# A perceiver block's graph stage: half of the batches sorted by GpSimd transfers with computed addresses, in place of one-hot products

## The chip, the core and the metric

One core of a Trainium2 chip runs the whole program. The metric is the device time of one execution in microseconds, as the median of several runs. The engines are TensorE (PE, with its weight loads PEld apart), VectorE (DVE), ScalarE (ACT), GpSimd (POOL) and SyncE (SP), which issues nearly all transfers of the kernel before. Each takes its instructions in order and waits for others through semaphores.

## The reference, cut to what matters

The input x has 16 batches of 32 channels and 512 nodes; the context gives three coordinates per node. The block adds three parts to x in turn: a graph stage, a state-space scan and a feed-forward part. Only the graph stage is touched. Its core, per layer:

```
keys  = [morton(q), morton(q_swapped), hilbert(q), hilbert(q_swapped)]
order = [argsort(k, axis=1) for k in keys]              # 4 methods, per batch
start = max(0, i - 5); end = min(N, i + 6)              # a window of 10 in sorted order
inds  = order[min(start + arange(10), end - 1)]
neigh = feats[inds]                                     # features of the window
x     = concat(center, neigh - center), channels permuted over methods, cast to float16
scores = einsum('bihd,bjhd->bhij', x, x) / sqrt(32)     # per node, 10 x 10, heads of 32
out   = softmax(scores) @ x                             # then a linear layer, a conv, instance norm, max
```

So each layer needs the node features of every batch put into the sorted order of each of four methods. There are two layers; the second takes the first one's output. The order is the same in both.

## The kernel before, in words

The work is split in four groups `g` of four batches (4 x 32 channels fill the 128 partitions) and two layers, eight passes in the order (0,L1) (1,L1) (0,L2) (2,L1) (1,L2) (3,L1) (2,L2) (3,L2). L1 has 32 output channels per batch, L2 has 64. A pass has 43 blocks of 12 nodes, 344 blocks in all, run as a software pipeline: the main loop (`for it in range(len(blocks) + 5)`, at the end of `graph_part`) issues for each `it` one step each of several blocks. In the order of the program: the exponential of block it-1 (`expo`, L870 and L875), `turn` of it-3 (L896), `scores` of it (L846, L853), `rest` and `reduce` of older blocks (L960 to L969), `greatest` (`c`, L862), `mapped` (L915, L920), `sums` (`z`, L882), then `steps`, which advances the preparation of the next pass, then `shares` of it-1 (`rz` on VectorE, L888, and `EN` on GpSimd, L890), `outputs` of it-3 (L943), and `differences` of block it+6 (`DD` on GpSimd, L811, and its copies `DX`, four transfers on SP per three blocks, L821). `EN` is thus read two iterations after it is issued, `DD` six after; `LEAD` is 6. Nothing reorders the instructions (`manual_schedule`).

The sorted position of each node comes from comparisons of keys: a TensorE product (L540) and a sign with accumulated sum on ScalarE (L541) give `rank`, one instruction pair for 128 nodes of one batch and method. `rank` holds 2 x position - 511. There are 256 such pairs; 32 are done before the first preparation starts, and `ranks_of(b)` tells how many must be done before batch b can be placed.

A preparation `prep(g, layer)` is a generator that brings one pass's features into sorted order. It stores the source in DRAM (`dC`), turns it on TensorE into `FT` (nodes on partitions, L641 and L643), splits `FT` into three bfloat16 parts `F3` (L648, L650), makes the linear part of the centre (`share`), and then for each of the four batches and four chunks of 128 nodes makes four one-hot matrices on VectorE (L751, one per method, 128x512) and multiplies the three parts by each on TensorE (L705, 12 products of 32 columns by 512). After four chunks ScalarE copies the result (L712), SP stores it to DRAM (L716), loads the centres `crep` (four transfers, L681) and loads the sorted features back as `fs`, spread over partitions by head (four transfers, L725). Each call of `next` runs it to its next `yield`: two one-hots per step.

`steps` calls the next pass's preparation once per block, or twice while more steps are left than `NGRP - LEAD - SPARE - gi`, which is 34 less the block number `gi`. The counts come from `PREP`: 49 steps for a preparation of L1, 46 for L2. From the second pass on it starts at block 4 at the earliest; while the former pass's end (`tails`) still runs, one step per block or none. A preparation that yields False (ranks not there yet) does not count a step. The first preparation runs alone, before block 1, with a rank comparison per step.

Of the kernel before, what the change touches and what calls it, by code (L numbers as in the profile page):

```python
# [8 lines left out]
F32 = mybir.dt.float32  # L9
F16 = mybir.dt.float16  # L10
# [13 lines left out]
M = 4  # L24
# [21 lines left out]
NHT = 16  # L46
LR = 18
LEAD = 6
PREP = (49, 46, 42)
SPARE = 3  # L50


# [325 lines left out]
def graph_part(nc, tc, cx, I, dram, id32, ones, xt, F0, layernorm_steps, rstd_steps, scan_input):  # L378
# [62 lines left out]

    EN = [keep.tile([P, NI, 32], F32, name=f"EN{k}") for k in range(2)]
    rank = keep.tile([P, 4, M, B], F32, name="rank")
    F1 = [keep.tile([P, D], F32, name=f"F1_{g}") for g in range(NBG)]

    W3 = gc.tile([P, 4, P], F32, name="W3")
# [100 lines left out]
    def ranks_of(b):  # L547

        return FIRST // 2 + HALF * (b + 1) if b < 4 else 4 * M * (b + 1)
# [70 lines left out]
    def later_tile(n):  # L620
        return ps_1.tile([P, D], F32, tag="misc", bufs=2, name=f"kd{n}")

    KEPT = ()
    kept = {}
    transfers = []

    def prep(g, layer, early=False):


        L, co, npair, WA, WC, HB = layers[layer]  # L630
        key = f"{L}_{g}"
        src = F1[g] if layer else F0[:, g]
        if layer == 0:
            yield from layernorm_steps(sm, src, xt[:, g], f"g{g}")
            yield
        dC = dram.tile([P, D], F32, name=f"dC{key}")
        nc.sync.dma_start(out=dC, in_=src)

        pf = ps_1.tile([P, 4, P], F32, tag="misc", bufs=2, name=f"pf{key}")
        for c in range(4):  # L640
            nc.tensor.transpose(pf[:, c], src[:, c * P:(c + 1) * P], id32)  # L641
        FT = wk.tile([P, 4, P], F32, tag="FT", name=f"FT{key}", bufs=1)
        nc.scalar.copy(FT, pf)  # L643
        yield

        F3 = [wk.tile([P, 4, P], BF16, tag=f"F3_{k}", name=f"F3_{k}{key}", bufs=1) for k in range(3)]
        for k in range(3):
            nc.vector.tensor_copy(F3[k], FT)  # L648
            if k < 2:
                nc.vector.tensor_tensor(FT, FT, F3[k], ALU.subtract)  # L650
                yield
        at_hand = layer == 1 and g in KEPT

        def share():

            c16 = wk.tile([P, D], F16, tag="c16", name=f"c16{key}", bufs=1)
            nc.vector.tensor_copy(c16, src)
            yield
            c32 = wk.tile([P, D], F32, tag="c32", name=f"c32{key}", bufs=1)
            nc.vector.tensor_copy(c32, c16)  # L660
            yield
            yield
            hc = wk.tile([P, npair, D], F32, tag="hc", name=f"hc{key}")
            for pr in range(npair):
                ph = ps_1.tile([P, D], F32, tag="misc", bufs=2, name=f"ph{key}_{pr}")
                nc.tensor.matmul(ph, lhsT=WC[:, pr], rhs=c32, start=True, stop=True)
                nc.scalar.activation(hc[:, pr], ph, AF.Identity, bias=HB)
                yield
            made[key][2] = hc

        made[key] = [None, None, None]
        if not at_hand:
            yield from share()

        crep = big.tile([P, 4, D], F32, tag="crep", name=f"crep{key}", bufs=2)
        later = []

        def centre(b):
            for m in range(M):
                r = 32 * b + 8 * m  # L680
                nc.sync.dma_start(  # L681
                    out=crep[r:r + 8], in_=dC[32 * b:32 * b + 32].rearrange("(h c) n -> c h n", h=4)
                )

        if early:
# [12 lines left out]
        fs = big.tile([P, 4, D + 4], F32, tag="fs", name=f"fs{key}", bufs=2)  # L698
        pend = []

        def place():
            b, c, ohs, pp = pend.pop(0)
            for m in range(M):
                for k in range(3):
                    nc.tensor.matmul(  # L705
                        pp[32 * m:32 * m + 32, :], lhsT=F3[k][:, c, 32 * b:32 * b + 32], rhs=ohs[m // 2][:, m % 2],
                        start=(c == 0 and k == 0), stop=(c == 3 and k == 2),
                    )
# [12 lines left out]

            def spread():
                for m in range(M):
                    r = 32 * b + 8 * m
                    nc.sync.dma_start(  # L725
                        out=fs[r:r + 8, :, :D], in_=dS[32 * m:32 * m + 32].rearrange("(h c) n -> c h n", h=4)
                    )

            later.append([2, store])

        for b in range(4):
            while ranked[0] < ranks_of(4 * g + b):
                yield False
            pp = None
            for c in range(4):
                if c == 0:
                    pp = ps_1.tile([P, D], F32, tag="pp", name=f"pp{key}_{b}")
                if at_hand and len(pend) == 2:
                    place()
                    tick()  # L740
                    yield
                ohs = [
                    wk.tile([P, 2, D], BF16, tag="oh", name=f"oh{key}_{b}_{c}_{i}", bufs=4) for i in range(2)
                ]
                for i, oh in enumerate(ohs):
                    if at_hand:
                        transfers.append((oh, kept[g, b, c, i]))
                        continue
                    for j in range(2):
                        m = 2 * i + j  # L750
                        nc.vector.tensor_scalar(  # L751
                            oh[:, j], it2, rank[:, c, m, 4 * g + b:4 * g + b + 1], None, ALU.is_equal
                        )
                    if layer == 0 and g in KEPT:
                        kept[g, b, c, i] = dram.tile([P, 2, D], BF16, name=f"k{key}_{b}_{c}_{i}")

                        def keep_it(to=kept[g, b, c, i], oh=oh):
                            nc.scalar.dma_start(out=to, in_=oh)

                        later.append([1, keep_it])  # L760
                    if i == 0:
                        tick()
                        yield
                if pend and not at_hand:
                    place()
                pend.append((b, c, ohs, pp))
                tick()
                yield
        while pend:
            place()  # L770
            tick()
            yield
        if at_hand:
            for _ in share():
                tick()
                yield
        while later:
            tick()
            yield
        made[key][:2] = fs, crep  # L780
# [230 lines left out]
    def finish(g, F2):  # L1011
        p3 = ps_1.tile([P, D], F32, tag="misc", bufs=2, name=f"p3_{g}")
        for j, f in enumerate((F0[:, g], F1[g], *F2)):
            nc.tensor.matmul(p3, lhsT=W3[:, j], rhs=f, start=(j == 0), stop=(j == 3))
        h3 = wk.tile([P, D], F32, tag="h3", name=f"h3_{g}", bufs=1)
        nc.scalar.copy(h3, p3)
        yield
        n3 = wk.tile([P, D], F32, tag="n3", name=f"n3_{g}", bufs=1)
# [19 lines left out]
    for gi in range(LEAD):  # L1038
        differences(0, gi)

    def at_hand(at):
        g, layer = order[at]
        return layer == 1 and g in KEPT

    def steps(at, gi):


# [7 lines left out]
        if at + 1 >= len(order):  # L1055
            return
        if at + 1 not in ahead:
            if at > 0 and gi < 4 and not at_hand(at + 1):
                return
            g, layer = order[at + 1]  # L1060
            ahead[at + 1] = [prep(g, layer), PREP[layer + at_hand(at + 1)]]
# [12 lines left out]
    for it in range(len(blocks) + 5):  # L1074
# [6 lines left out]
        if gi == 0 and it < len(blocks):  # L1081
            begin(at)
        do(expo, 1)
        for oh, of in transfers:
            nc.scalar.dma_start(out=oh, in_=of)
        transfers.clear()
        do(turn, 3)
        do(scores, 0)
        do(rest, 5)
# [584 lines left out]
```

## Time and profile before

| what | value |
|---|---|
| median of 3 runs | 2288.53 us (2284.22 to 2291.29) |
| profiled execution, its own time | 2296.19 us |
| its span | 2294.1 us |
| blocks of the graph stage (first and last `c`) | 110.4 to 1290.0 us |
| PE, DVE, ACT, POOL busy, share of the span | 92%, 78%, 50%, 36% |
| the same between 110 and 1300 us | 1115.8, 1077.4, 688.6, 684.0 of 1190 us |
| granted TensorE clock, whole span | 0.978 |
| one-hots (L751) | 512 instructions, 155.9 us busy in the page's groups |
| their products (L705) | 1536 instructions, 110.5 us busy |
| `DX` loads on SP, 128 pieces of 720 B | median 0.60 us to issue |
| loads of `wing` on SP, 128 pieces of 2 KB | median 0.33 us to issue |
| transfers issued by GpSimd | none |

The page gives busy time per engine over the whole span, which mixes the graph stage with two others. Its second part cuts the span into 40 slices of 57.35 us, with the busy share in tenths. A timeline lists single instructions with start, duration, engine and line; a bracket behind a line tells how long the engine stood idle before it and what ended the wait. Consecutive instructions of VectorE overlap by some 0.1 us, so the time that one takes of the engine is the distance between starts. DMA issues are not counted as busy.

### The profile page before, as it was taken

How to read it: one execution, taken by the hardware profiler on the slowest of the kernel's cores; microseconds unless marked ns; L12 is line 12 of the kernel's file. 1: busy time of each engine (PE TensorE's matmuls, PEld its weight loads, DVE VectorE, ACT ScalarE, POOL GpSimd, SP SyncE). 2: the span in 40 equal slices, each digit the busy share in tenths (PEclk: the TensorE clock that was granted, in tenths of full speed). 3: DMA queues.
4: the chain of work that ended last, by engine and by line, in shares of the span. 5: the costliest groups of instructions: out<-in, count | busy, mean ns of one | idle time of the engine just before them, and what ended most of it. 6: DMA issues, size and time to landing. Idle time of an engine off the chain costs nothing. (4 is left out here: it accounts for less than half of the span.)

```text
span 2294.1 us, 91947 instructions
## 1 busy us (share of the span) xinstructions
PE 2099.9 (92%) x40610; PEld 1274.3 (56%) x40610; DVE 1796.4 (78%) x3976; ACT 1140.7 (50%) x2073; POOL 831.4 (36%) x905
## 2 busy tenths in 40 slices
PE   5598899999999998889999789979999999999979
PEld 2255555776556775567777544446556465564422
DVE  8488897999989999989999854596876867765543
ACT  6686576556665554355555323343543534435321
POOL 2156656556565565665655300110211211111200
PEclk9899999999999999999999889989999999999989
DMA  1323232141232321423211122212131221311110
GB/s 47 80 61 81 53 76 64 45 93 45 57 79 47 77 57 41 98 47 73 61 36 37 28 73 71 69 58 88 36 99 51 60 88 41 94 52 55 38 37 19
DMA packets 121637, 138.18 MB, mean 60 GB/s; under 512 B 18398, under 2 KB 79506, under 8 KB 121154
## 3 DMA queue, kind: packets, MB, share of 16 engines
q1 hardware_dynamic: 121240, 132.32, 22.9%
q8 instruction: 319, 5.23, 1.0%
q14 instruction: 78, 0.64, 0.1%
HBM read 77.02 MB, written 12.85 MB: 39 GB/s over the span
## 5 line engine op out<-in xcount | busy, mean ns | idle before, releaser
L890 POOL TENSOR_TENSOR EN<-e,rz 128x480 f32<-128x480 f32 x344 | 342.3, 995 | 501.6 <-DVE rz L888 408.4
L915 PE MATMUL u<-WA,DD 128*32 128x128 bf16 (+1 forms) x16512 | 412.8, 247 | 21.1 <-issue 20.8
L920 ACT COPY us<-u 128x512 f32<-128x512 f32 x516 | 301.7, 586 | 157.1 <-PE u L915 140.7
L915 PEld LDWEIGHTS <-DD 128*32 128x32 f16 x16512 | 337.5, 97 | 55.3 <-issue 53.5
L875 ACT ACTIVATE e<-s,smc 128x480 f32<-128x480 f32 x344 | 227.3, 661 | 250.5 <-PE s L870 219.6
L811 POOL TENSOR_TENSOR DD<-fs,crep 128x480 f16<-128x480 f32 (+2 forms) x344 | 349.5, 1017 | 0.0
L943 PEld LDWEIGHTS h<-e,us 128*32 128x32 f32 (+1 forms) x11008 | 245.9, 125 | 133.0 <-issue 66.4
L943 PE MATMUL h<-e,us 128*32 128x30 f32 (+1 forms) x11008 | 278.8, 210 | 30.5 <-issue 12.8
L1377 POOL TENSOR_TENSOR ssq<-ssq,sq 128x512 f32<-128x512 f32 x56 | 79.6, 1421 | 582.3 <-ACT sq L1376 582.3
L862 DVE TENSOR_REDUCE c<-s 128x16 bf16<-128x480 f32 x344 | 220.8, 642 | 87.3 <-PE s L853 83.8
L1184 PE MATMUL ppg<-hT,wing 128*128 128x512 f32 x512 | 238.4, 609 | 0.0
L1184 PE MATMUL ppch<-hT,winch 128*128 128x512 f32 x512 | 230.9, 593 | 1.1 <-ACT gs L1272 1.1
L1197 DVE SCALAR_TENSOR_TENSOR cyh<-ppch,t_conv_w,cyh 128x496 f32<-128x496 f32 (+2 forms) x192 | 137.6, 717 | 119.8 <-ACT cyh L1191 115.3
L896 DVE STREAM_TRANSPOSE e<-EN 128x512 f32<-128x512 f32 x344 | 224.8, 654 | 0.0
L882 DVE TENSOR_REDUCE z<-e 128x16 f32<-128x480 f32 x344 | 219.8, 639 | 0.4 <-ACT e L875 0.4
L541 ACT ACTIVATE sgn<-kd 128x512 bf16<-128x512 f32 x256 | 153.1, 598 | 52.3 <-PE kd L540 49.3
L853 PEld LDWEIGHTS <-DD 128*32 128x32 f16 x5504 | 81.0, 96 | 159.1 <-issue 132.2
L751 DVE TENSOR_SCALAR oh<-it,rank 128x512 bf16<-128x512 f16 x512 | 155.9, 365 | 8.5 <-PE pp L705 8.5
L853 PE MATMUL s<-DX,DD 128*32 128x120 f16 x5504 | 142.4, 221 | 19.5 <-DMA DX<-DD 15.5
L1184 PEld LDWEIGHTS ppch<-hT,winch 128*128 128x128 f32 x512 | 94.3, 190 | 111.4 <-issue 101.7
L1184 PEld LDWEIGHTS ppg<-hT,wing 128*128 128x128 f32 x512 | 94.5, 192 | 101.8 <-issue 98.1
L870 PE MATMUL s<-c,idb 128*128 128x480 bf16 x344 | 130.3, 379 | 5.2 <-DVE c L862 2.7
(372 smaller groups left out, 3057.8 us busy)
## 6 DMA issues: line engine op xcount, KB each, us to landing
DX<-DD SPq DMA_DIRECT2D x456, 90.0 KB
wing<-in_in_proj SPq DMA_DIRECT2D x64, 256.0 KB
winch<-in_in_proj SPq DMA_DIRECT2D x64, 256.0 KB
wo<-in_out_proj SPq DMA_DIRECT2D x64, 256.0 KB
crep<-dC SPq DMA_DIRECT2D x128, 64.0 KB
dS<-so SPq DMA_DIRECT2D x32, 256.0 KB
fs<-dS SPq DMA_DIRECT2D x128, 64.0 KB
wincB<-in_in_proj SPq DMA_DIRECT2D x8, 256.0 KB
```

What stands on the lines that cost most here:

```text
L751: nc.vector.tensor_scalar(oh[:, j], it2, rank[:, c, m, 4 * g + b:4 * g + b + 1], None, ALU.is_equal)
L811: nc.gpsimd.tensor_tensor(d[:, :, m0 - n0:n1 - n0], win, crep[:, :, m0:n1].unsqueeze(3).to_broadcast([P, 4, n1 - m0, K]), ALU.subtract,)
L853: nc.tensor.matmul(s[rh, j * 4 * QB:(j + 1) * 4 * QB].rearrange("p (b q) -> p b q", b=4), lhsT=d[:, h, c0:c0 + 32], rhs=dx[:, h, :, c0:c0 ...
L862: nc.vector.tensor_reduce(c, live["s", at, gi].rearrange("p (i q) -> p i q", q=QB), AX.X, ALU.max, negate=True)
L875: nc.scalar.activation(e, s.rearrange("p (i q) -> p i q", q=QB), AF.Exp, scale=smc)
L882: nc.vector.tensor_reduce(z, e, AX.X, ALU.add)
L890: nc.gpsimd.tensor_tensor(en[:, :, :QB], e, rz.unsqueeze(2).to_broadcast([P, NI, QB]), ALU.mult)
L896: nc.vector.transpose(e.rearrange("p i q -> p (i q)"), en.rearrange("p i q -> p (i q)"))
L915: nc.tensor.matmul(u[rh, jj], lhsT=d[:, h, c0:c0 + 32], rhs=WA[k][:, h].rearrange("p b o -> p (b o)"), start=(jj == 0 and k == 0), stop=(k ...
L920: nc.scalar.copy(us[:, j - jj:j + 1], u)
L943: nc.tensor.matmul(h[r:r + co, pr, q0:q0 + QB], lhsT=us[:, j, b * co:(b + 1) * co], rhs=e[:, 4 * j + b, :QB], start=npair > 1, stop=True, ...
L1184: nc.tensor.matmul(pp, lhsT=w[:, k], rhs=hT[:, k], start=(k == 0), stop=(k == 3))
```

## The change

Batches 2 and 3 of each group stay with one-hots. Batches 0 and 1 are sorted by GpSimd: for each batch, chunk and method one indirect transfer writes 128 rows of 32 features (128 bytes each) from `FT` to a DRAM tile `box`, at the row that `place_of` names; that is 32 transfers per preparation. `place_of` is worked out from `rank` in the L1 preparation, in one instruction per batch, and kept for L2. Then SP loads the eight boxes back (`rows`, 512 pieces of 128 bytes each), ScalarE copies them into the head-wise order (`sorted_`, eight copies), TensorE turns them (16 float32 transposes) and ScalarE copies the result into `fs` (four copies of 64x512). The two generators advance together, one step of each per call. `F3` is made for batches 2 and 3 alone. `PREP` goes from (49, 46, 42) to (41, 38, 42). Two stores and eight loads per preparation go with the one-hots of batches 0 and 1. Some tiles share a buffer (`c16` with `sorted_`, `c32` with `rows`, `n3` with `lr`), the one-hot buffers go from four to three, and an unused path that kept one-hots in DRAM (`KEPT`, `at_hand`) goes.

The diff, cut to its core:

```diff
-PREP = (49, 46, 42)
+PREP = (41, 38, 42)
...
+    place_of = keep.tile([P, NBG, 2, 4, M], I32, name="place_of")
+    turned = keep.tile([P, 4, M], F32, name="turned")
+    nc.vector.memset(turned, (D - 1) / 2)
...
-        F3 = [wk.tile([P, 4, P], BF16, tag=f"F3_{k}", name=f"F3_{k}{key}", bufs=1) for k in range(3)]
+        F3 = [wk.tile([P, 4, 64], BF16, tag=f"F3_{k}", name=f"F3_{k}{key}", bufs=1) for k in range(3)]
         for k in range(3):
-            nc.vector.tensor_copy(F3[k], FT)
+            nc.vector.tensor_copy(F3[k], FT[:, :, 64:])
...
-        for b in range(4):
-            while ranked[0] < ranks_of(4 * g + b):
+        def one_hots():
+            for b in (2, 3):
+                while ranked[0] < ranks_of(4 * g + b):
+                    yield False
...
+                    for i, oh in enumerate(ohs):
+                        for j in range(2):
+                            m = 2 * i + j
+                            nc.vector.tensor_scalar(
+                                oh[:, j], it2, rank[:, c, m, 4 * g + b:4 * g + b + 1], None, ALU.is_equal
+                            )
+                        if i == 0:
+                            yield
+                    if pend:
+                        place()
+                    pend.append((b, c, ohs, pp))
+                    yield
...
+        def scattered():
+            at = place_of[:, g]
+            boxes = [[dram.tile([D, 32], F32, name=f"box{key}_{b}_{m}") for m in range(M)] for b in range(2)]
+            while ranked[0] < ranks_of(4 * g + 1):
                 yield False
+            for b in range(2):
+                if layer == 0:
+                    nc.vector.scalar_tensor_tensor(
+                        at[:, b], rank[:, :, :, 4 * g + b], 0.5, turned, ALU.mult, ALU.add
+                    )
             for c in range(4):
+                for b in range(2):
+                    for m in range(M):
+                        nc.gpsimd.indirect_dma_start(
+                            out=boxes[b][m],
+                            out_offset=bass.IndirectOffsetOnAxis(ap=at[:, b, c, m:m + 1], axis=0),
+                            in_=FT[:, c, 32 * b:32 * b + 32], in_offset=None,
                         )
+                        if m % 2:
+                            yield
+            yield
+            rows = wk.tile([P, 2, 4, M, 32], F32, tag="rows", name=f"rows{key}", bufs=1)
+            for b in range(2):
+                for m in range(M):
+                    nc.sync.dma_start(
+                        out=rows[:, b, :, m], in_=boxes[b][m].rearrange("(c p) f -> p c f", c=4)
+                    )
+                if not early:
+                    centre(b)
                 yield
+            for _ in range(2):
+                yield
+            sorted_ = wk.tile([P, 4, 4, 2, M, 8], F32, tag="sorted", name=f"sorted{key}", bufs=1)
+            for c in range(4):
+                for b in range(2):
+                    nc.scalar.copy(
+                        sorted_[:, c, :, b], rows[:, b, c].rearrange("p m (h k) -> p h m k", h=4)
+                    )
+                yield
+            for h in range(4):
+                pt = ps_1.tile([P, D], F32, tag="misc", bufs=2, name=f"pt{key}_{h}")[:64]
+                for c in range(4):
+                    nc.tensor.transpose(
+                        pt[:, c * P:(c + 1) * P], sorted_[:, c, h].rearrange("p b m k -> p (b m k)"), id32
+                    )
+                nc.scalar.copy(fs[:64, h, :D], pt)
+                yield
+
+        running = [scattered(), one_hots()]
+        while running:
+            got = [next(t, t) for t in running]
+            running = [t for t, r in zip(running, got) if r is not t]
             tick()
+            yield False if all(r is False for r in got) else None
```

More of the change, by code (lines that the diff above doesn't have):

```diff
@@ L621, in later_tile @@
         return ps_1.tile([P, D], F32, tag="misc", bufs=2, name=f"kd{n}")
-    KEPT = ()
-    kept = {}
-    transfers = []
     def prep(g, layer, early=False):
@@ L644, in prep @@
         yield
-        F3 = [wk.tile([P, 4, P], BF16, tag=f"F3_{k}", name=f"F3_{k}{key}", bufs=1) for k in range(3)]
+        F3 = [wk.tile([P, 4, 64], BF16, tag=f"F3_{k}", name=f"F3_{k}{key}", bufs=1) for k in range(3)]
         for k in range(3):
-            nc.vector.tensor_copy(F3[k], FT)
+            nc.vector.tensor_copy(F3[k], FT[:, :, 64:])
             if k < 2:
-                nc.vector.tensor_tensor(FT, FT, F3[k], ALU.subtract)
+                nc.vector.tensor_tensor(FT[:, :, 64:], FT[:, :, 64:], F3[k], ALU.subtract)
                 yield
-        at_hand = layer == 1 and g in KEPT
         def share():
-            c16 = wk.tile([P, D], F16, tag="c16", name=f"c16{key}", bufs=1)
+            c16 = wk.tile([P, D], F16, tag="sorted", name=f"c16{key}", bufs=1)
             nc.vector.tensor_copy(c16, src)
             yield
-            c32 = wk.tile([P, D], F32, tag="c32", name=f"c32{key}", bufs=1)
+            c32 = wk.tile([P, D], F32, tag="rows", name=f"c32{key}", bufs=1)
             nc.vector.tensor_copy(c32, c16)
@@ L671, in prep @@
         made[key] = [None, None, None]
-        if not at_hand:
-            yield from share()
+        yield from share()
         crep = big.tile([P, 4, D], F32, tag="crep", name=f"crep{key}", bufs=2)
@@ L705, in place @@
                     nc.tensor.matmul(
-                        pp[32 * m:32 * m + 32, :], lhsT=F3[k][:, c, 32 * b:32 * b + 32], rhs=ohs[m // 2][:, m % 2],
+                        pp[32 * m:32 * m + 32, :], lhsT=F3[k][:, c, 32 * b - 64:32 * b - 32], rhs=ohs[m // 2][:, m % 2],
                         start=(c == 0 and k == 0), stop=(c == 3 and k == 2),
@@ L729, in place @@
             later.append([2, store])
-        for b in range(4):
-            while ranked[0] < ranks_of(4 * g + b):
-                yield False
-            pp = None
-            for c in range(4):
[L736 to L752, printed above, removed]
-                        )
[L754 to L767, printed above, removed]
-                yield
@@ L769, in prep @@
-        while pend:
-            place()
-            tick()
[L772 to L776, printed above, removed]
+        def one_hots():
+            for b in (2, 3):
+                while ranked[0] < ranks_of(4 * g + b):
+                    yield False
+                pp = None
+                for c in range(4):
+                    if c == 0:
+                        pp = ps_1.tile([P, D], F32, tag="pp", name=f"pp{key}_{b}")
+                    ohs = [
+                        wk.tile([P, 2, D], BF16, tag="oh", name=f"oh{key}_{b}_{c}_{i}", bufs=3) for i in range(2)
+                    ]
+                    for i, oh in enumerate(ohs):
[10 more added lines that the diff above has]
+                    yield
+            while pend:
+                place()
+                yield
@@ new lines, in scattered @@
+        def scattered():
+            at = place_of[:, g]
+            boxes = [[dram.tile([D, 32], F32, name=f"box{key}_{b}_{m}") for m in range(M)] for b in range(2)]
+            while ranked[0] < ranks_of(4 * g + 1):
+                yield False
+            for b in range(2):
[3 more added lines that the diff above has]
+                    )
+            for c in range(4):
+                for b in range(2):
[4 more added lines that the diff above has]
+                            in_=FT[:, c, 32 * b:32 * b + 32], in_offset=None,
+                        )
+                        if m % 2:
[9 more added lines that the diff above has]
+                    centre(b)
+                yield
+            for _ in range(2):
[9 more added lines that the diff above has]
+                pt = ps_1.tile([P, D], F32, tag="misc", bufs=2, name=f"pt{key}_{h}")[:64]
+                for c in range(4):
+                    nc.tensor.transpose(
+                        pt[:, c * P:(c + 1) * P], sorted_[:, c, h].rearrange("p b m k -> p (b m k)"), id32
+                    )
+                nc.scalar.copy(fs[:64, h, :D], pt)
+                yield
@@ L1017, in finish @@
         yield
-        n3 = wk.tile([P, D], F32, tag="n3", name=f"n3_{g}", bufs=1)
+        n3 = wk.tile([P, D], F32, tag="lr", name=f"n3_{g}", bufs=1)
         yield from layernorm_steps(sm, n3, h3, f"f{g}")
@@ L1039, in graph_part @@
         differences(0, gi)
-    def at_hand(at):
-        g, layer = order[at]
-        return layer == 1 and g in KEPT
     def steps(at, gi):
@@ L1057, in steps @@
         if at + 1 not in ahead:
-            if at > 0 and gi < 4 and not at_hand(at + 1):
+            if at > 0 and gi < 4:
                 return
             g, layer = order[at + 1]
-            ahead[at + 1] = [prep(g, layer), PREP[layer + at_hand(at + 1)]]
+            ahead[at + 1] = [prep(g, layer), PREP[layer]]
         a = ahead[at + 1]
@@ L1083, in graph_part @@
         do(expo, 1)
-        for oh, of in transfers:
-            nc.scalar.dma_start(out=oh, in_=of)
-        transfers.clear()
         do(turn, 3)
```

## The prediction

> **What bounds the kernel now.** I read the page's 40 slices first (57.35 us each), then each engine's timeline in single blocks of the graph stage, then the operation groups.
>
> ```profile
> PE   5598899999999998889999789979999999999979
> ...
> DVE  8488897999989999989999854596876867765543
> ...
> POOL 2156656556565565665655300110211211111200
> ```
>
> The graph stage is the first 23 slices: block 1 starts at 110.4 us, the last at 1290.0 (starts of `c`, L862). There TensorE and VectorE stand at 8 or 9 tenths, GpSimd at 5 or 6. The stretch behind it is not touched. Busy shares do not say which engine ends a block, so here is TensorE in one block of the wide layer (L2) beside the one-hots, start and duration in us:
>
> ```profile
> 456.72 0.38 PE L870 MATMUL s<-c,idb 128*128 128x480 bf16 x1
> 456.94 0.37 PE L846 MATMUL s<-mR,mL 128*128 128x480 bf16 x1
> 457.23 0.40 PE L853 MATMUL s<-DX,DD 128*32 128x120 f16 x16
> 457.46 1.48 PE L915 MATMUL u<-WA,DD 128*32 128x256 bf16 x48
> 458.77 0.82 PE L705 MATMUL pp<-oh,F 128*32 128x512 bf16 x12
> 459.52 1.12 PE L943 MATMUL h<-e,us 128*64 128x30 f32 x32
> 460.58 0.38 PE L870 MATMUL s<-c,idb 128*128 128x480 bf16 x1
> ```
>
> No gap: 3.86 us from one L870 to the next, 0.75 of them (458.77 to 459.52) for the one-hot product. VectorE beside it:
>
> ```profile
> 456.70 0.66 DVE L896 STREAM_TRANSPOSE e<-EN 128x512 f32<-128x512 f32 x1
> 457.28 0.62 DVE L960 TENSOR_TENSOR hs<-h,hc 128x480 f32<-128x480 f32 x1
> 457.93 0.41 DVE L969 BATCH_NORM_STATS2 stats<-hs 128x6 f32<-128x240 f32 x1
> 458.26 0.64 DVE L862 TENSOR_REDUCE c<-s 128x16 bf16<-128x480 f32 x1
> 458.82 0.64 DVE L882 TENSOR_REDUCE z<-e 128x16 f32<-128x480 f32 x1
> 459.38 1.13 DVE L751 TENSOR_SCALAR oh<-it,rank 128x512 bf16<-128x512 f16 x4
> 460.42 0.25 DVE L888 RECIPROCAL rz<-z 128x16 f32<-128x16 f32 x1
> ```
>
> No gap either; the four one-hots take 1.04 (459.38 to 460.42). Both engines bind. The mean of such blocks is 3.82 us. Later in the same pass, without one-hots, L870 follows L870 after 3.21 us:
>
> ```profile
> 521.60 0.38 PE L870 MATMUL s<-c,idb 128*128 128x480 bf16 x1
> ...
> 524.81 0.38 PE L870 MATMUL s<-c,idb 128*128 128x480 bf16 x1
> ```
>
> So a block's one-hot work is worth 0.61 us, not 1.04: TensorE is next. In passes of the narrow layer (L1) the starts of L862 give 3.44 with one-hots (13.76 per four blocks) and 3.05 without (36.5 for twelve), so 0.39. GpSimd in the first block:
>
> ```profile
> 456.96 0.99 POOL L890 TENSOR_TENSOR EN<-e,rz 128x480 f32<-128x480 f32 x1 [1.75 <-DVE rz L888]
> 457.91 1.04 POOL L811 TENSOR_TENSOR DD<-fs,crep 128x480 f16<-128x480 f32 x1
> ```
>
> The two are 2.0 us of work to the end of `DD` at 458.95, and 1.75 idle stood before them. `EN` ends at 457.95 and is turned two blocks later (456.70 + 2 x 3.86 = 464.4): some 6 us of lead.
>
> **What goes.** 64 one-hots per preparation become 32. A step still makes two, and a double step four per block, so a block with one-hots is as heavy as before; there are 8 of them and no longer 16. That is worth 8 x 0.61 = 4.9 us in the three preparations beside an L2 pass, 8 x 0.39 = 3.1 in the four beside an L1 pass: 27 us. This is all that VectorE and TensorE can give outside the start. The casts and subtractions of `F3` at half width: 3 x 0.47 + 2 x 0.69 = 2.8 us become some 1.6; much of it lies in unbound blocks: -4 for seven.
>
> **What comes to TensorE and ScalarE.** 16 float32 transposes per preparation. The row for four of them at the start (L641) is 1.09 us; in the stretch 200 to 1200 the row has 16 in 2.6 us, 0.16 each. TensorE binds the blocks without one-hots, so 16 x 0.16 x 7 = +18. ScalarE gets eight copies of 128x128 and four of 64x512 (0.59 by L712) for two `so` copies, some 4 us over eight steps; at half load, nothing.
>
> **What comes to GpSimd: 32 indirect transfers per preparation, price X each.** The instruction stream is in order, so they stand before `EN` and `DD` of the block. No row shows one. Bounds by rows: below, the issue of a plain 128-piece transfer on SP, 0.33 us (`wing`); above, GpSimd's longest elementwise instruction on 128x512, 1.42 (`ssq`, L1377). All GpSimd rows that take two 128x480 or 128x512 operands lie between 0.995 and 1.42; I take X = 1.1, between `EN` (0.995) and `da` (1.208), because the work is done by this engine and for 128 partitions. By the counts of steps (38 or 41 to do by block 34, double steps while more is left than blocks) the transfers fall, four a block, into about 7 blocks, and two a block into 2 more. Excess over the present block:
> L2: 7 x (2.0 + 4.4 - 3.82) + 2 x (2.0 + 2.2 - 3.5) = 19.5, less 6 of lead, 13.5.
> L1: 7 x (2.0 + 4.4 - 3.44) + 2 x (2.0 + 2.2 - 3.2) = 22.7, less 6, 16.7.
> Net of what goes: 3 x (13.5 - 4.9) + 4 x (16.7 - 3.1) = 26 + 54 = **+80**. In these blocks the turn (L896) waits for `EN`, and behind it on VectorE `c`, `z` and the reductions, hence TensorE. Each 0.1 us of X is 25.6 us over eight preparations.
>
> **The start.** The first preparation has no blocks beside it. Batches 0 and 1 need 48 rank comparisons; the 48th ends at 78.1 (L541). 32 X = 35.2 gives 113.3. From the last `so` copy (95.46) to the first `DD` (103.26) two passes through DRAM take 7.8; again two, and then 16 transposes with copies, 5: 126 against 103.3. **+23** (at X = 0.33: none).
>
> **The way back.** SP issues eight loads of 512 pieces for two stores and eight loads. Rows: 32 pieces 0.31 us (`crep`), 128 pieces 0.60 (`DX`); at that slope 512 are 1.75, at one per 128 pieces 2.4, and no less than 0.33. The copies on ScalarE come some four blocks, 13 us, behind the first load; eight loads at 1.75, the centres (8 x 0.31) and 2 to land are 18.5. In front of a late copy stand `e` and `us`, which TensorE needs. Between 0 and 13 us a preparation; I take 2, as ScalarE is idle near half the time: **+14**. On SP, `DX` waits behind the loads; it has four blocks in hand.
>
> **Sum:** 80 + 18 - 4 + 23 + 14 = +131. The profiled execution took 2296.2 us (span 2294.1), 7.7 above the median of 2288.5; against the median: **2420 us**, slower by 5.7%.
>
> **Rows and the Trainium skill.** Four one-hots take 1.51 us at 607.96, where a `DD` of GpSimd runs beside them until 608.53, and 1.12 at 605.09, where none does. "SBUF — State Buffer", Who interferes with whom, says that such VectorE instructions and GpSimd lock each other out, and, under Two separate sides, that a GpSimd transfer of 620 ns took 3100 beside a copy, since its descriptors could not be written. By 3.1 us the sum would be about +640, an estimate; our rows show a loss of 0.4 per four. "DMA: Bandwidth & Descriptors", Anatomy of one DMA, puts the fixed cost at 2.0 us, mostly at completion, off the engine; if all of it held the engine, 25.6 x 9 = 230 would come on top. Its Rules for kernel authors speak against 16 KB pieces altogether.
>
> **Rivals.**
> 1. *Cheap issue, faster.* GpSimd only hands work on, as SP does at 0.33 to 0.60. With 32X - 12.5 (L1) and 32X - 15.7 (L2) against 6 us of lead, bursts cost nothing below X = 0.58 and 0.68, and the whole sum turns at about 0.6. At 0.45: -27 + 18 - 4 + 2 = -11: 2277; with the transposes hidden 2260. For it: SP's rows, and 1.8 free us per block. Against it: every GpSimd row of this size. 0.15.
> 2. *Dearer transfers*: one-hots and transfers hold each other up, X = 1.5 to 1.9: 2520 to 2625. For it: 1.51 against 1.12. Against: GpSimd's `EN` keeps 0.995 in all blocks. 0.22.
> 3. *The way back binds*: X near 0.6, so the sum is near 0, and 13 late us seven times, 91: 2290 to 2380. For it: 512 pieces per load; against: SP is mostly idle. 0.11.
> My forecast, X from 0.8 to 1.45, 2340 to 2510: 0.52.
>
> The range 2280 to 2600 leaves out the best of rival 1 and the end of rival 2. 0.3% (7 us) is what a measurement can tell here. Faster 0.13, the same 0.05 (rivals 1 and 3 near zero), slower 0.82.
>
> **What would show it.** Blocks of 6.4 us for seven blocks of each pass, with `EN` back to back with transfers, VectorE waiting at L896 for GpSimd, TensorE down in those blocks; blocks of 3.2 (L2) just after. First `DD` at about 126. No long wait of ScalarE for `rows`. Wrong, if blocks beside the transfers stay at 3.8 or if the waits name DMA.

## The result and the profile after

The changed kernel takes **2495.9 us** (median of 4, 2494.3 to 2497.3) against 2289.9 for the kernel before beside it: a ratio of 1.0903, interval [1.0880, 1.0926]. The prediction was 2420, with a range of 2280 to 2600. The sign and the mechanism hold; the size is 76 us short. The profiled execution has a span of 2495.0 us, 200.9 more than before (2294.1). All differences below are of these two spans, in which 70 of the 76 us lie; the other 6 come mostly from the profiled execution of before, which took 6.3 us more than its median, where that of the changed kernel took 0.9 more.

The slices of the page of the changed kernel (62.4 us each):

```profile
PE   5476786989978979858889995997999999999979
...
DVE  8254776778966867957879996449778678675533
...
POOL 2468577676576675676766550011111111111200
```

The graph stage is now the first 24 slices. VectorE and TensorE no longer stand at 8 and 9 throughout: they sink in one or two slices of each pass, and GpSimd rises to 7 or 8 there. The dips lie where the transfers are. GpSimd's timeline in one of them, beside a pass of L2 (L922 and L843 are `EN` and `DD`, L768 is the transfer):

```profile
884.65 1.00 POOL L922 TENSOR_TENSOR EN<-e,rz 128x480 f32<-128x480 f32 x1
885.60 1.03 POOL L843 TENSOR_TENSOR DD<-fs,crep 128x480 f16<-128x480 f32 x1
886.80 1.01 POOL L768 DMA_INDIRECT box<-FT,place_of  x1 [0.17 <-issue]
888.11 0.95 POOL L768 DMA_INDIRECT box<-FT,place_of  x1 [0.30 <-issue]
889.37 0.96 POOL L768 DMA_INDIRECT box<-FT,place_of  x1 [0.31 <-issue]
890.63 0.96 POOL L768 DMA_INDIRECT box<-FT,place_of  x1 [0.30 <-issue]
891.61 1.01 POOL L922 TENSOR_TENSOR EN<-e,rz 128x480 f32<-128x480 f32 x1
```

GpSimd stands still nowhere but for the 0.30 us ahead of each transfer, and those belong to it: starts are 1.26 us apart (888.11 to 889.37), though one is busy for 0.96. From `EN` to `EN` are 6.96 us, and this is the period of the whole pipeline. VectorE in the same stretch waits at the turn, as the prediction said:

```profile
885.68 0.71 DVE L928 STREAM_TRANSPOSE e<-EN 128x512 f32<-128x512 f32 x1 [2.79 <-POOL EN L922]
```

In the list of waits of the graph stage (who waited for whom: us in total, times, longest) the changed kernel has a line that the kernel before has not:

```profile
DVE e L928 <- POOL EN L922: 160.0, 47, 7.0
```

I took the starts of `c` (L862 before, L894 after) as the block boundaries of both traces and subtracted block by block. The prediction's terms stand beside it:

| part of the span | predicted | measured |
|---|---|---|
| until the first `c` | +23 | +23.4 (110.4 to 133.8) |
| 64 blocks with transfers (the "bursts"), and those of a pass ahead of them | +107 (149 less 42 of lead) | +156.9 (+164.2 and -7.3) |
| blocks behind them: one-hots gone, `F3`, transposes, way back | +1 (-27 - 4 + 18 + 14) | +22.4 |
| behind the graph stage | 0 | -1.7 |
| sum | +131 | +201 |

Two terms fall short: the bursts by 50 us, the blocks behind them by 21. The second moves a little from run to run: by the same subtraction the two later runs with the same order of instructions (the changed kernel again, and twice the bytes) have +24.6 and +26.4 there, and +164.2 and +164.0 in the bursts.

### The profile page after: what moved, and what is told of

Same layout as the page of the kernel before. It is cut to its first block, busy times and chain, and to the rows that moved or that the text cites. A ratio compares the mean times of both kernels' runs of the same rounds, so it can differ in the third digit from the quotient of the medians.

```text
span 2495.0 us, 90813 instructions
## 1 busy us (share of the span) xinstructions
PE 2134.7 (86%) x39928; PEld 1296.3 (52%) x39970; DVE 1756.0 (70%) x3729; ACT 1159.5 (46%) x2153; POOL 1080.9 (43%) x1161
## 5 line engine op out<-in xcount | busy, mean ns | idle before, releaser
L922 POOL TENSOR_TENSOR EN<-e,rz 128x480 f32<-128x480 f32 x344 | 343.0, 997 | 391.4 <-DVE rz L920 301.7
L947 PE MATMUL u<-WA,DD 128*32 128x128 bf16 (+1 forms) x16512 | 435.7, 257 | 23.0 <-issue 22.4
L947 PEld LDWEIGHTS <-DD 128*32 128x32 f16 x16512 | 354.1, 102 | 53.7 <-issue 45.7
L843 POOL TENSOR_TENSOR DD<-fs,crep 128x480 f16<-128x480 f32 (+2 forms) x344 | 349.3, 1016 | 0.0
L768 POOL DMA_INDIRECT box<-FT,place_of x256 | 250.3, 978 | 129.5 <-issue 60.0
L894 DVE TENSOR_REDUCE c<-s 128x16 bf16<-128x480 f32 x344 | 220.8, 642 | 120.2 <-PE s L885 117.8
L885 PEld LDWEIGHTS <-DD 128*32 128x32 f16 x5504 | 84.8, 99 | 195.9 <-issue 166.6
L885 PE MATMUL s<-DX,DD 128*32 128x120 f16 x5504 | 148.3, 229 | 43.8 <-DMA DX<-DD 38.1
```

Source lines behind the costliest of these rows:

```text
L768: nc.gpsimd.indirect_dma_start(out=boxes[b][m], out_offset=bass.IndirectOffsetOnAxis(ap=at[:, b, c, m:m + 1], axis=0), in_=FT[:, c, 32 * b ...
L843: nc.gpsimd.tensor_tensor(d[:, :, m0 - n0:n1 - n0], win, crep[:, :, m0:n1].unsqueeze(3).to_broadcast([P, 4, n1 - m0, K]), ALU.subtract,)
L885: nc.tensor.matmul(s[rh, j * 4 * QB:(j + 1) * 4 * QB].rearrange("p (b q) -> p b q", b=4), lhsT=d[:, h, c0:c0 + 32], rhs=dx[:, h, :, c0:c0 ...
L894: nc.vector.tensor_reduce(c, live["s", at, gi].rearrange("p (i q) -> p i q", q=QB), AX.X, ALU.max, negate=True)
L922: nc.gpsimd.tensor_tensor(en[:, :, :QB], e, rz.unsqueeze(2).to_broadcast([P, NI, QB]), ALU.mult)
L947: nc.tensor.matmul(u[rh, jj], lhsT=d[:, h, c0:c0 + 32], rhs=WA[k][:, h].rearrange("p b o -> p (b o)"), start=(jj == 0 and k == 0), stop=(k ...
```

## The experiments

The main theory, **A**: a burst block is the sum of GpSimd's own instructions, and a transfer holds GpSimd for 1.26 us. Its rivals are the order on GpSimd (C), a way back that binds (D, E, F, G), and a price that goes with bytes. There are twelve runs.

### Without GpSimd's transfers

```diff
-                        nc.gpsimd.indirect_dma_start(
-                            out=boxes[b][m],
-                            out_offset=bass.IndirectOffsetOnAxis(ap=at[:, b, c, m:m + 1], axis=0),
-                            in_=FT[:, c, 32 * b:32 * b + 32], in_offset=None,
-                        )
+                        nc.sync.dma_start(
+                            out=boxes[b][m][c * P:(c + 1) * P], in_=FT[:, c, 32 * b:32 * b + 32]
+                        )
```

> Leaves the sorting out: the 32 transfers of a preparation go to the same boxes with the same 128 pieces of 128 bytes each, but in node order, as plain transfers that SP issues. All else is the changed kernel. Theory A (an indirect transfer holds GpSimd for 1.26 us, 0.96 busy and 0.30 before the next; with EN and DD, 2.0, a block with four takes 7.0): the blocks beside the transfers fall from 7.0 to 3.4 to 3.8, so the 164 us that these stretches cost go, and of the 23 at the start most (32 x 0.4 us on SP in place of 32 x 1.26); the way back stays. 2290 to 2330 us. Rival B (the cost is in the memory: 4096 writes and 4096 reads of 128 bytes, and the transposes and copies after them): at least 2430.

Measured: 2334.9 us, ratio 1.0175 [1.0146, 1.0204], just outside the expected interval. The blocks beside the stores are back to 3.75 to 3.88 us (L2), so some 161 of the 206 us go with GpSimd's transfers. But 40 us remain, though VectorE and TensorE do half of the one-hot work: +7.8 ahead of the first `c`, +34.5 in the stage. The latter sit in single blocks, most of them behind the stores, of 6.2 to 11.3 us where 3.1 to 3.9 are usual, and the waits name `DX` (TensorE's waits):

```profile
PE s L883 <- DMA DX<-DD: 59.5, 16, 12.9
```

Of these, 12.9 us stand ahead of the first block, so 46.6 are in the stage. Before, this wait is at 15.5 us, 14.6 of them ahead of the first block, so 0.9 in the stage. A part of the 40 us belongs to the substitute itself: SP now issues the 32 stores, and of the 21 copies `DX` whose issue starts over 1 us after their `DD` ended, 7 have such stores in front of them on SP's queue.

### Half of the transfers

```diff
+                        if m < 2:
                             nc.gpsimd.indirect_dma_start(
...
+                        else:
+                            nc.sync.dma_start(
+                                out=boxes[b][m][c * P:(c + 1) * P], in_=FT[:, c, 32 * b:32 * b + 32]
+                            )
```

> Leaves half of the sorting out: methods 0 and 1 by GpSimd's indirect transfers as in the changed kernel, methods 2 and 3 as plain transfers in node order from SP. Theory A: a block then has two of 1.26 us, 2.0 + 2.5 = 4.5, against 3.4 to 3.8: an excess of 0.7 to 1.1 in seven blocks, of which the 6 us lead of EN covers most. The stretches cost 10 to 25 us in all and not 164, the start 10 to 15 less: 2320 to 2350 us. If the cost were in proportion to the number of transfers (no threshold): about 2400.

Measured: 2383.7 us, ratio 1.0396 [1.0364, 1.0428], above the 2350 that I had put at the top; most blocks with transfers last 3.6 to 5.7 us. By the line from 2334.9 to 2495.9 half would be 2415, so the half costs less than half: two transfers a block use more of GpSimd's free time. The number is blurred by pauses of TensorE (42.6 us inside single lines in these blocks), of which more below.

### Twice as many blocks with half as many transfers each

```diff
-PREP = (41, 38, 42)
+PREP = (57, 54, 42)
...
-                        if m % 2:
-                            yield
+                        yield
```

> Two transfers per block in place of four, over twice as many blocks; the counts of steps are set to match, so that the rest of the preparation keeps its place. Theory A (GpSimd's stream is the bound of the bursts; a transfer costs 1.26 us of it): blocks of 2.0 + 2 x 1.26 = 4.5 us, 16 per preparation. Against blocks of 3.82 (L2) and 3.44 (L1) that is 5.0 us less the 6 us lead in half of them; the excess of a preparation falls from 13.7 to about 5 beside L2 and from 18.8 to about 11 beside L1: some 55 us less over seven preparations, 2440 within 15. Rival (only the number of transfers counts, since GpSimd has no idle time to give in these blocks): within 10 of the unaltered run.

Measured: **2416.6**, ratio 1.0541 [1.0499, 1.0584], 79 us below the changed kernel with the same 256 transfers. The rival (only their number counts) falls. GpSimd in a block of it:

```profile
844.51 1.01 POOL L921 TENSOR_TENSOR EN<-e,rz 128x480 f32<-128x480 f32 x1
...
846.66 1.01 POOL L768 DMA_INDIRECT box<-FT,place_of  x1 [0.17 <-issue]
847.98 0.96 POOL L768 DMA_INDIRECT box<-FT,place_of  x1 [0.31 <-DVE rz L919]
848.95 1.01 POOL L921 TENSOR_TENSOR EN<-e,rz 128x480 f32<-128x480 f32 x1
```

4.44 us from `EN` to `EN`, against 4.5 expected and 6.96 above: the difference is two transfers of 1.26. Blocks with transfers cost +83.4 us in place of +164.2. I had expected 55 less and got 81. The transfers now lie in 116 blocks in place of 64, and each of the 52 more gives GpSimd's free time, which is 1.2 to 1.8 us (blocks of 3.2 to 3.82, less 2.0); 81 / 52 is 1.6.

Behind the bursts this kernel stands at +26.4 us, and there the stall is another one than in the changed kernel below. ScalarE takes its instructions in order, and its copies of `rows` come before the loads have landed; `e` waits behind them, and TensorE for `e` (L789 the copies, L906 `e`):

```profile
568.58 0.30 ACT L789 COPY sorted<-rows 128x128 f32<-128x128 f32 x1 [6.27 <-DMA rows<-box]
568.78 0.66 ACT L906 ACTIVATE e<-s,smc 128x480 f32<-128x480 f32 x1
569.49 0.56 PE L877 MATMUL s<-mR,mL 128*128 128x480 bf16 x1 [3.44 <-ACT e L906]
```

In the stage this wait of TensorE for `e` sums to 17.0 us here and to 0.9 in the changed kernel; its wait for `DX` is 5.6 here and 26.1 there.

### Behind `EN` and `DD`

```diff
+        for move in moves:
+            move()
+        moves.clear()
     for t in (*tails, scan_input(sm, junk(NBG - 1), NBG - 1)):
```

Here, in all preparations but the first, `scattered` only collects the transfers of a block, and they are issued at its end.

> The same 32 transfers, issued behind EN and DD of their block and no longer ahead of them. Theory A (throughput of GpSimd's queue): blocks stay at 7.0 us and the time within 8 us of 2496. Rival C (only the order hurts: EN is late because four transfers stand before it in the same block, and two blocks of lead would do if it went first): the blocks fall to below 5, the time to 2410 or less.

> The kernel with the transfers behind EN and DD once more (2533.3 on another chip than the control run), to tell the chip from the edit. If the edit makes the pauses of TensorE inside single lines (98 us in the bursts, against 3.8 in the control run): 2533 within 10, with pauses of 80 us or more. If that chip made them: 2490 to 2510, with pauses under 20 us.

Measured: 2533.3, ratio 1.1036 [1.1003, 1.1070], and on another chip 2544.0, 1.1094 [1.1062, 1.1127]. Rival C falls: in this order too GpSimd's six instructions, `EN`, `DD` and four transfers, fill 6.99 us from one `EN` to the next (910.50 to 917.49 in the second of these runs). Both totals are dearer than the changed kernel and lie outside theory A's 2496 within 8; with them go pauses of TensorE of 98 and 106 us inside single lines, on both chips. See the end of this part.

### Twice the bytes

```diff
-            boxes = [[dram.tile([D, 32], F32, name=f"box{key}_{b}_{m}") for m in range(M)] for b in range(2)]
+            boxes = [[dram.tile([D, 64], F32, name=f"box{key}_{b}_{m}") for m in range(M)] for b in range(2)]
...
-                            in_=FT[:, c, 32 * b:32 * b + 32], in_offset=None,
+                            in_=FT[:, c, 32 * b:32 * b + 64], in_offset=None,
```

> Each indirect transfer carries rows of 64 columns (256 bytes) in place of 32; the loads of the boxes take the first 32 columns as before, so the result and every other instruction stay. If the 1.26 us of GpSimd are for the 128 rows (or fixed), the price and the time stay: 2496 within 10, or within 10 of the unaltered run. If they go with the bytes moved, a transfer takes 1.9 to 2.5 us and the time is 2650 or more.

Measured: 2497.0, ratio 1.0889 [1.0845, 1.0932], no difference from 2495.9. The row of the transfers in this run (least, median and greatest duration in ns):

```profile
L768 POOL DMA_INDIRECT box<-FT,place_of x256: 954/958/1277, 71.1 to 1271.7; - x128
```

With rows of 128 bytes the median is 959. The price does not go with the bytes. Whether it goes with the 128 rows or is fixed was not tried.

### The changed kernel again

> The changed kernel once more, unaltered, as the bound for the others of this call. If the pauses of TensorE inside single lines (some 97 us in the bursts of the two runs that put transfers behind EN and rows on ScalarE, none of note in the changed kernel's first profile) and its granted clock of 0.63 to 0.86 there come from those edits, this run gives 2496 within 8 and a clock of 0.74 to 0.94 in the bursts. If they come from the chip on which they ran, this run shows them too and lies at 2530 to 2560.

Measured: 2498.7, ratio 1.0897 [1.0854, 1.0940], with 3.8 us of pauses of TensorE inside single lines in the bursts. The runs with two a block and with twice the bytes, on the same chip, had 10.3 and 3.3.

### The way back: rows on another queue, spread out, and more lead

```diff
-                    nc.sync.dma_start(
+                    nc.scalar.dma_start(
                         out=rows[:, b, :, m], in_=boxes[b][m].rearrange("(c p) f -> p c f", c=4)
```

> The eight loads of rows are issued from ScalarE's queue and no longer from SP's. Theory D (after the transfers, the scores wait for DX because SP issues the loads of rows and the centres ahead of it: 6 us of TensorE and then some us at a lower clock): these stalls, 4 to 10 us in five of the passes, mostly go: 2465 to 2485 us. Rival E (DX is late in the memory's queues, behind 2048 pieces of 128 bytes, whoever issues them): within 6 us of 2496, or slower by the issue time on ScalarE (8 x 0.5 us a preparation).

Measured: 2562.5, ratio 1.1157 [1.1118, 1.1197]. Theory D gets nothing from it. The run has 96.9 us of pauses in its bursts, so its total says little; behind the bursts, where the rows are loaded, it stands at +32, and the changed kernel at +22. TensorE's waits for `DX` in the stage are 24.1 us, against 26.1 in the changed kernel. Moving the rows off SP did not help.

```diff
-PREP = (41, 38, 42)
+PREP = (47, 44, 42)
...
-                if not early:
-                    centre(b)
-                yield
+                    if not early:
+                        centre(b, (m,))
+                    yield
```

This is the run with plain stores, with one load of rows and one of centres per step.

> Leaves the sorting of batches 0 and 1 out, as the run with plain transfers from SP did (2334.9), and issues one load of rows and one of centres per step, over eight steps, in place of four and four in two steps; the counts of steps go up by six. Theory D (the way back costs because the copies DX stand behind up to sixteen loads on SP's queue): the waits of TensorE and GpSimd for DX after the bursts go, 2305 or less. Rival E (the loads themselves are slow, with 4096 pieces of 128 bytes in the memory queues, wherever they are issued): 2328 or more, with the same waits on DMA.

Measured: 2344.3, ratio 1.0210 [1.0156, 1.0263], against 2334.9 without the spread. D as I had put it, a clump on SP, falls too: with the loads spread over eight steps, 19 copies `DX` start over 1 us late, against 21 without the spread, and TensorE's waits for them in the stage are 36.5 us, against 46.6. The time is in rival E's range, but whether the loads are slow by themselves was not separated. What both leave standing is the question how much `DX` has in hand. Here is the changed kernel behind a burst, in order of time (SPq is SP's queue; L678 the centres, L853 the copies `DX`, L885 the scores that read them):

```profile
927.35 3.24 SPq L779 DMA_DIRECT2D rows<-box  x4
928.31 1.03 POOL L843 TENSOR_TENSOR DD<-fs,crep 128x480 f16<-128x480 f32 x1
...
930.64 1.44 SPq L678 DMA_DIRECT2D crep<-dC  x4
...
932.18 4.28 SPq L853 DMA_DIRECT2D DX<-DD  x4
...
938.26 0.59 PE L885 MATMUL s<-DX,DD 128*32 128x120 f16 x16 [6.07 <-DMA DX<-DD]
```

`DD` ends at 929.34, and SP gets to its `DX` at 932.18, behind four loads of rows and four of centres. The issue ends at 936.46, the data are used at 938.26, and TensorE has stood for 6.07 us. Over all triples of blocks, in the kernel before: from the end of `DD` to the use of its `DX` are 8.5 us in the median; the issue takes 2.5 to 3.6 of them, and in the changed kernel about 1.7 pass from its end to the earliest use after a wait. So `DX` has some 4 us in hand. Before, its issue starts over 1 us late in 2 of 114 cases, after the change in 11, by up to 5.0.

```diff
-LEAD = 6
+LEAD = 7
...
-SPARE = 3
+SPARE = 2
```

> Leaves the sorting of batches 0 and 1 out: plain transfers from SP as in the first run of this kind (2334.9, of which 34.5 us lie in the blocks behind the stores), with seven blocks of lead. Theory F: half or more of the 34.5 goes, 2300 to 2318. Rival G: 2328 or more.

> DD and its copies DX are made seven blocks ahead in place of six (SPARE goes from 3 to 2, so that the preparation keeps its steps); nothing else. Theory F (the stalls behind the bursts come because DX has little in hand: in the changed kernel TensorE uses it a median of 8.9 us after its DD ends, and issue and landing take some 5 of them, while the loads of the way back hold up the issue by 1 to 5 us in eleven cases): one more block, 3 us, covers most of that; the waits of TensorE for DX (38.1 us) and of GpSimd for DX (15.1) shrink to under 15 together, and the time to 2465 to 2482. Rival G (the loads land late wherever DX stands, and fs or the rows bind next): 2488 or more.

> Two transfers per block (2416.6 by itself) together with seven blocks of lead. Theory F: 2395 to 2405. Rival G: 2412 or more. In any case above the kernel before, since the start alone is 18 us later and 32 x 1.26 us of GpSimd per preparation stay.

With plain stores: 2324.6, ratio 1.0152 [1.0119, 1.0186]. The time lies between the two expectations, but the stage falls from +34.5 to +15.4, by more than half, while the first block comes 2.4 later (seven `DD` ahead of it). TensorE's waits for `DX` fall to

```profile
PE s L883 <- DMA DX<-DD: 35.5, 8, 12.9
```

which is 22.6 in the stage, against 46.6. In the changed kernel with this lead the same wait is at

```profile
PE s L885 <- DMA DX<-DD: 15.8, 3, 11.7
```

where it was 38.1; in the stage that is 4.1 for 26.1. (GpSimd's wait for `DX` says little: 2.6 here, 15.1 and 34.1 in the two runs of the changed kernel, 24.6 before.) The blocks behind the bursts go from +22.4 to -3.6. As a total, though, this kernel takes 2542.8 (1.1093 [1.1058, 1.1129]), and the one with two transfers a block 2482.4 (1.0831 [1.0796, 1.0866]). Both are slower than without the lead, so theory F's totals fail. They lie in rival G's open ranges. In the first of the two that is not for G's reason, as the waits for `DX` and for `rows` both shrink (`rows` on ScalarE to 6.4 us from 16.4); the excess lies in its bursts.

What this shows of theory F is therefore limited. The clean pair is the one with plain stores: 24 us less waiting for `DX`, 19 us less in the stage. In the changed kernel the 26 us cannot all be put down to the lead, as its run has the pauses of TensorE that come next, and the two runs with the transfers behind `EN`, with the same pauses and six blocks of lead, stand at +5.0 and +4.4 behind their bursts (the one with rows on ScalarE, with pauses too, at +32). With two transfers a block the lead gives next to nothing there, +24.7 in place of +26.4. In that kernel the wait for `rows` on ScalarE binds, as G has it: TensorE's wait for `e` stays, at 20.7 us for 17.0.

**What stays open.** The excess of these two is in the bursts (+227.2 in place of +164.2; +126.7 in place of +83.4), where TensorE stops in the midst of a line, mostly for 0.3 to 1.1 us, waiting for nothing that the trace shows. In the second run with the transfers behind `EN`:

```profile
908.45 0.26 PE L893 MATMUL s<-DX,DD 128*32 128x120 f16 x4 [0.49 <-issue]
909.20 0.28 PE L893 MATMUL s<-DX,DD 128*32 128x120 f16 x5 [0.49 <-issue]
909.96 0.25 PE L893 MATMUL s<-DX,DD 128*32 128x120 f16 x4 [0.48 <-issue]
```

The stops lie in the bursts; in the rest of the stage every run has 18 to 32 us of such pauses, and the kernel before has 37 in the whole of it. Within a burst they do not keep to the transfers: in the four kernels with four a block, 62 to 66% of the stopped time lies under a transfer of GpSimd, and transfers fill 62 to 64% of these bursts. Five runs have 90 to 117 us in the bursts (behind `EN` twice, rows on ScalarE, and both with GpSimd's transfers and more lead), the half of the transfers 42.6; the changed kernel, its second run, two a block and twice the bytes have 2 to 10, and the three with plain stores alone 6 to 8. The edits are a poor explanation: the start shows the same, where the changed kernel and the one with more lead issue the same instructions up to the first `DD`. There, of the kernel with more lead:

```profile
104.65 1.70 PE L702 MATMUL pp<-oh,F 128*32 128x512 bf16 x6 [10.29 <-issue]
```

Its 64th rank comparison ends at 119.7 us; in the changed kernel at 89.8. The kernels that stop ran on two chips, the control run and its two companions on a third. Whether the chip decides, or where the program lies in memory, was not separated: the control run was not made on the first two chips, and the chip of the changed kernel's first run is not on record. The three kernels with plain stores alone ran one on each of these chips. So totals with stops (2482 to 2563) are not set against totals without, and what I use of those runs is the part behind the bursts.

## Why the prediction was right in kind and 76 us short

- **The mechanism, right.** GpSimd's stream bounds the blocks with transfers; `EN` stands back to back with them, VectorE waits at the turn (160.0 us), TensorE sinks. Removing the transfers takes away 161 us, and pacing them 79. Of the signs that the prediction named, blocks of 6.4 us came out at 6.96; the first `DD` and the short blocks just after came as said (2.8 to 3.1 us beside L2). "No long wait of ScalarE for `rows`" did not hold: 16.4 us in five waits in the stage, up to 4.8. And behind the bursts the waits do name DMA, 26.1 us of TensorE for `DX`, one wait in each of the seven passes.
- **The price X, mis-sized**: 1.1 taken, 1.26 measured from start to start (medians of 1.26 to 1.32 over the runs), whether 128 or 256 bytes per row. This is the largest share: 25.6 us for each 0.1 make 41, of which 36 are in the bursts and 5 at the start. With it alone the sum would have given 2461. I took the rows of GpSimd's arithmetic as the likeness, and an instruction of 0.96 is near them; what I left out is the 0.30 us until the next one starts. The Trainium skill, "Perfetto Trace Analysis", section DMA Instruction — SWDGE (GPSIMD), says that such a record ends when the descriptors are written, not when the data have moved. The runs agree: the record stays at 958 ns with twice the data, while a transfer lands 2.2 us after its issue (median).
- **The lead of `EN`, too kind.** With X = 1.26 the formula gives 3 x 24.6 + 4 x 27.8 = 185 gross; measured are 156.9, the blocks ahead of the bursts included, so the lead is worth 4.0 us a preparation and not 6. That makes 14, and with the 36 the 50 by which the bursts fall short.
- **The way back, where the step failed.** The term took 2 us a preparation, for ScalarE alone, and these blocks came out 21 us dearer. "On SP, `DX` waits behind the loads; it has four blocks in hand." It has some 4 us, little more than one block: from the end of `DD` to the use there are 8.5 and not four blocks of 3.2 to 3.8, since `DD` stands behind `EN`, and `EN` waits for `rz` at the end of the block; the issue and the landing take the rest. One more block of lead took 19 us out of the stage of the kernel with plain stores, where the pair is clean. The step that the prediction looked at, ScalarE's copies of `rows`, is late as well; it binds once the transfers are paced. How the 21 us divide between the two was not measured.
- **What goes, and the transposes: right beside L2.** In the plain run with more lead the three passes of L2 with a preparation change by -2.2, -2.4 and -3.6 us; the prediction's terms, without the 2 for the way back, give -4.9 - 0.6 + 2.6 = -2.9. Only the sum is confirmed; the single terms were not taken apart. Beside L1 they give -1.1, and +4 to +11 were measured: all of the 22.6 us of waiting for `DX` are in these passes.
- **The start, right by luck**: first `DD` at 126.63 for 126. The transfers began at 72.03, not after the 48th comparison (77.2 in this run), since batch 0 needs the first 40 alone (71.5), and took 41 us in place of 35, which cancels. And the last link is another one than was forecast:

```profile
117.67 0.57 ACT L709 COPY so<-pp 128x512 f32<-128x512 f32 x1
122.07 1.30 SPq L722 DMA_DIRECT2D fs<-dS  x4
126.63 0.24 POOL L832 TENSOR_TENSOR DD<-fs,crep 128x24 f16<-128x24 f32 x1 [13.70 <-DMA kr<-others]
```

  The way of GpSimd's transfers, with the turn, was done when the last copy into `fs` ended at 121.44. What came last is the half that stayed with one-hots: the products of batch 3 end at 95.49, but its copy `so` stands behind ScalarE's copies of `rows` and comes at 117.67, and then its own pass through DRAM follows. Its last load is issued at 123.4, and `DD` starts 3.3 us later; in the kernel before 3.9 us lie between the two. So up to 5 us of the +23.4 are the place of one copy in the program. (The bracket names `kr`, the last event before; `DD` reads `fs`.)
- **Not foreseen: TensorE's clock.** In the windows of a burst beside L2 it falls from 1.00 to 0.85 (third column from the right; the others are the length, busy time by engine, and the DMA's share and rate). Before, and after:

```profile
435.00:470.00 35.00, 35.00 (x1026) 26.39 (x1018) 34.83 (x93) 18.16 (x31) 18.36 (x19) 1.00 0.30 64
```

```profile
517.00:574.00 57.00, 45.05 (x1052) 31.20 (x1042) 39.71 (x90) 18.88 (x32) 47.44 (x49) 0.85 0.20 44
```

  In the bursts it should cost nothing, as GpSimd sets the period; behind a stall it does: the `u` products at 938.61 take 2.80 us where 1.49 is usual, and the granted clock from 938.2 to 943.0 is 0.50.
- **The rivals.** The cheap issue (X below 0.6) and the dearer transfers (1.5 to 1.9) are both excluded by the 1.26 of starts. The way back binds a little at any X, not only near 0.6.

No version found here beats the kernel before. Even with the transfers taken off GpSimd and one more block of lead it is 1.5% slower, though that kernel has 32 stores per preparation on SP's queue in their place.

## What to carry to other kernels

A transfer with computed addresses is work of GpSimd's stream, 1.26 us here for 128 rows of 128 as of 256 bytes; before adding some, count GpSimd's free time per period of the pipeline, and issue no more per period than fits. Price an operation by the distance from one start to the next, not by its busy time. For a transfer that is "blocks ahead", measure the time from its producer's end to its use in the trace of before: four blocks in the program were 8.5 us in time here, some 4 of them to spare, and any load put in front of it on its queue spends them. The same holds for an engine that takes its instructions in order: a copy that waits for a late load holds up whatever stands behind it.

## What the runs showed of the hardware

- Twice the data per row changed neither a transfer's record on GpSimd (958 ns) nor the time (2497.0 against 2495.9).
- In the changed kernel 110 of the 256 transfers run beside a one-hot of VectorE; 102 of these records stay between 0.95 and 1.06 us, and 8 are longer, up to 1.28. The Trainium skill, "SBUF — State Buffer", SBUF: two separate sides, tells of one that grew from 620 to 3100 ns beside a copy; no run here shows anything like it (greatest record 1279 ns).
- TensorE's granted clock was lower in the bursts: 0.74 to 0.94 in seven stretches of the changed kernel, 0.93 to 1.00 at two transfers a block, 1.00 in the same stretches before. It does not follow the busy share alone: 0.94 at 45.86 us of 61, but 0.85 at 45.05 of 57, and 1.00 at 24.80 of 30 before.
- In some runs TensorE stops in the midst of lines in the blocks with GpSimd's transfers, 43 to 117 us in all, on two of three chips or in certain programs. The pairs 2544.0 against 2498.7 and 2482.4 against 2416.6 differ by 45 and 66 us, but by an edit too. It is not explained.
